# Two layers of windowed attention and experts on one core: another engine for a norm's root, and another way of spreading the score shifts

## The chip, the core and the metric

The kernel runs on one core of a Trainium2 chip. A core has TensorE (matrix products, in the profile PE for the products and PEld for the loading of their stationary operand), VectorE (DVE), ScalarE (ACT), GpSimd (POOL) and SyncE (SP, which here issues DMAs). Each engine works through its own instructions in order; semaphores let one wait for another. SBUF holds the operands, PSUM takes TensorE's results. The metric is the time of one execution on the device in microseconds (us). A kernel's time is the median of several executions, and one more execution is recorded by the hardware profiler.

## The reference: what is computed

The input `x` has 4 sequences of 512 tokens with 128 features. There are two layers, and each computes `x + s * silu(g)` from the normalised input `xn`. `s` comes from attention and `g` from eight experts, of which one is picked for each token.

```python
xn = _layernorm(x)
s = _L0_attn_ref(xn, ...)      # 16 heads of 8, causal window of 64, sigmoid-based weights
g = _silu(_L0_ffn_ref(xn, ...))
x = x + s * g
xn = _layernorm(x)
s = _L1_attn_ref(xn, ...)      # layernorm, blocks of 64 queries by 64 keys, then a feed forward
g = _silu(_L1_ffn_ref(xn, ...))
return x + s * g
```

In layer 1 the attention is cut into windows of 64 tokens that start every 32. Inside a window each of 64 queries sees all 64 keys; neighbouring windows are blended. Its output, projected and with its residual, goes through a second layernorm (`(x - m) / sqrt(v + eps)`), a dense layer to 512 features with gelu, and a dense layer back to 128:

```python
out = ctx @ wproj + bproj + residual
h = layernorm(out, ln2_g, ln2_b)
h = gelu(h @ w1 + b1, approximate=False) @ w2 + b2
return h + out
```

## The kernel before

**Tiles.** A sequence (`b`, four of them) is cut into four tiles of 128 tokens (`t`), so there are 16 attention tiles in each layer. The 16 heads are taken as 4 groups `g` of 32 partitions with 4 heads `j` each. The experts' tokens are sorted into 23 blocks of 128 for each layer.

**Stages and their order.** Every stage is a Python generator (`scores_q`, `queries1`, `scores_k1`, `values1`, `feed1`, the experts' `moe_x`, `moe_h`, `moe_y` and so on). `run` at the end of the function picks the next stage by a simple plan: a stage names the events that it needs (`yield "M", [...]`) and then books what it costs on TensorE and on the other engines (`spent(cost, steps, events)`, with steps such as `("D", 0.7)` for VectorE, `("G", 1.0)` for GpSimd and `(None, 0.9)` for time that belongs to no engine). The plan fixes the order of TensorE's instructions. The order on the other engines follows from the program's order, from a scheduler in the framework with its own costs, and from a few dependencies that `spent` adds where a step follows a GpSimd step. In `run` the plan also remembers a gap before a stage; `bank`, which hands out a PSUM bank, passes it to `awake`, and that fills the gap with products of ones whose result is overwritten. `bank16` hands out a bank for bf16 transpositions without that.

**A norm's root.** `rsqrt` (lines 389 to 393) adds eps on VectorE and takes the power -0.5 on GpSimd. `rsqrt_many` (lines 395 to 408) does the whole on VectorE, by a bit shift for a first guess and three Newton steps; before the change only layer 0's query and key norms (`project0`) use it, with 128 columns. `feed1` (lines 1413 to 1469) runs eight times, for two halves `u` of each sequence. It multiplies the context by `wproj` (`pr`), adds the residual, takes the moments `mv`, the root `rs`, and the normalised rows `hn` on VectorE (`centred`), then adds the row `ffn2` to the residual on GpSimd, transposes `hn` on TensorE (`tr_hn`) and goes on with the two dense layers (`f`, `fy`).

**GpSimd's other work in layer 1.** The gathers of the experts' tokens (`xb`, line 609), the scatters of their results (`yt`, line 666), and the queries masked by head (`q4`, line 1251).

**The shift of layer 1's scores.** The softmax needs each query's maximum subtracted from its scores. `queries1` computes a tile's scores with the queries on the partitions, two window offsets `par` (0 and 32 tokens), and for each the two blocks `w` of 64 queries on partitions `64w` to `64w+63`. VectorE takes the negated maxima `mx` (line 1290) and `split` writes them as a sum of three bf16 terms into `shb` (lines 467 to 472), twelve columns (3 terms by 4 heads) in each group's 32. TensorE transposes `shb` (`tr_sh`), ScalarE copies it out (`shd`, line 1298), and four VectorE products with the 0/1 mask `smask` (line 1301) spread it over the heads: `sh4` has four heads by 128 queries for each `par`. `scores_k1` then computes the scores again with the keys on the partitions, and adds the shifts by products with ones:

```python
for w in range(2):
    for g in range(G):
        r = slice(32 * g, 32 * g + NS * J)
        mm(ps[g // 2][w * KB : (w + 1) * KB, g % 2, par], ones16[r, 0:KB],
           sh4[r, par, :, w * KB : (w + 1) * KB], start=False, stop=True)
```

That is 16 products a tile (2 `par`, 2 `w`, 4 `g`), each with 12 rows and 64 output columns, after 16 products of scores with 32 rows and 64 output columns (each two instructions in the profile). The exponential on ScalarE (`pt`, line 1333) follows. Layer 0 (`scores_k`) shifts its scores with 4 products a tile of 12 rows and 128 output columns.

Of the kernel before, what the change touches and what calls it, by code (L numbers as in the profile page):

```python
# [16 lines left out]
P = 128  # L17
# [3 lines left out]
G, J = 4, 4  # L21
# [36 lines left out]
def two_layers(  # L58
# [336 lines left out]
    def rsqrt_many(dst, src, scale, eps):  # L395

        n = dst.shape[1]
        x = small.tile([P, n], F32, tag="rq_x", name=f"rq_x_{dst.tensor.name}", bufs=1)
        nc.vector.tensor_scalar(x, src, scale, eps, ALU.mult, ALU.add)
        y = small.tile([P, n], F32, tag="rq_y", name=f"rq_y_{dst.tensor.name}", bufs=1)  # L400
        nc.vector.tensor_single_scalar(y.bitcast(I32), x.bitcast(I32), 1, ALU.logical_shift_right)
        nc.vector.tensor_scalar(y.bitcast(I32), y.bitcast(I32), -1.0, float(0x5F3759DF), ALU.mult, ALU.add)
        nc.vector.tensor_scalar_mul(x, x, -0.5)
        z = small.tile([P, n], F32, tag="rq_z", name=f"rq_z_{dst.tensor.name}", bufs=1)
        for i in range(3):
            nc.vector.tensor_tensor(z, y, y, ALU.mult)
            nc.vector.tensor_tensor(z, z, x, ALU.mult)
            nc.vector.scalar_tensor_tensor(dst if i == 2 else y, z, 1.5, y, ALU.add, ALU.mult)
# [50 lines left out]
    def transposed16(src, n, name):  # L459
        ps = bank16(f"tr_{name}")  # L460
        for t in range(n):
            turn(ps[:, t * P : (t + 1) * P], src[:, t], ident16)
        return ps[:, 0 : n * P]
# [446 lines left out]
    for i in range(2):  # L910
        nc.gpsimd.tensor_copy(
            ves[i][:, 0 : H * VC].rearrange("p (h d) -> p h d", d=VC)[:, :, HD], valid[:, i : i + 1].to_broadcast([P, H])
        )
    shbs1 = prepared("shb1_", 2, [P, 2, G, 32], BF16)
    later.close()


# [63 lines left out]
    def scores_q():  # L981

        for i in range(NTILE):
            b, t = divmod(i, NT)
            yield "S", [("k4", b), ("qd", b), ("fit", b - 2)]
            if t == 0:
                mxs[b] = (
                    small.tile([P, NT, H], F32, tag="mx", name=f"mx_{b}"), small.tile([P, NT, H], F32, tag="sm", name=f"sm_{b}")
                )
            mx, sm = mxs[b]  # L990
            qd, k4 = qds[b], k4s[b]


            ps = [banks(f"s0_{b}_{t}_{gg}")[:, :, 0 : J * QW] for gg in range(2)]
            for g in range(G):

                r, eye = (slice(0, P), ident16) if t == 0 else (slice(32 * g, 32 * g + 32), diag32)
                band = band_q[r, 1 if t == 0 else 0, None].to_broadcast([r.stop - r.start, J, QW])
                mm(ps[g // 2][:, g % 2], eye[r], band, start=True, stop=False)
            for c in range(P // QB):  # L1000
                o = t * P + c * QB
                for g in range(G):
                    r = slice(32 * g, 32 * g + 32)
                    mm(
                        ps[g // 2][c * QB : (c + 1) * QB, g % 2], qd[r, o : o + QB], k4[r, :, o : o + QW],
                        start=False, stop=True,
                    )
            def over_keys(dst, src, gg, op):
                nc.vector.tensor_reduce(  # L1009
                    dst[:, t, 8 * gg : 8 * gg + 8].rearrange("p (u j) -> p u j", u=2),  # L1010
                    src.rearrange("p u (j f) -> p u j f", j=J), AX.X, op,
                )

            for gg in range(2):
                over_keys(mx, ps[gg], gg, ALU.max)
                th = att_p.tile([P, 2, J * QW], F32, tag="th", name=f"th_{b}_{t}_{gg}", bufs=2)
                nc.scalar.activation(th, ps[gg], AF.Tanh, scale=0.5 * SCALE)  # L1017
                over_keys(sm, th, gg, ALU.add)
                spent(0 if gg else 1.5, [("D", 0.95), ("A", 0.83), ("D", 0.95)], [("s0", i)], scores=2)
# [218 lines left out]
    def queries1():  # L1238


        for i in range(NTILE):
# [49 lines left out]
                    mx.rearrange("p a g j -> p g a j")[:, 2 * gg : 2 * gg + 2], ps[gg], AX.X, ALU.max, negate=True,  # L1291
                )
            shb = shbs1[i % 2]
            split(shb, mx, f"1_{b}_{t}")
            spent(1.15, [("D", 2.45), ("D", 1.0)], [("s1", i), ("shb", i)], scores=1)
            yield "M", [("shb", i), ("e1", i - 2)]
            shd = att_p.tile([P, 2 * P], BF16, tag="shd1", name=f"shd1_{b}_{t}")
            nc.scalar.copy(shd, transposed16(shb.rearrange("p a g r -> p a (g r)"), 2, f"sh1_{b}_{t}"))
            sh4 = att_p.tile([P, 2, J, P], BF16, tag="sh4_1", name=f"sh4_1_{b}_{t}")
            for j in range(J):  # L1300
                nc.vector.tensor_scalar_mul(sh4[:, :, j], shd.rearrange("p (a f) -> p a f", a=2), smask[:, j : j + 1])  # L1301
            asked1[i] = q4, sh4, v
            spent(0.13, [("A", 0.4), ("D", 1.2)], [("sh1", i)])

    def scores_k1():
        for i in range(NTILE):
            b, t = divmod(i, NT)
            yield "S", [("sh1", i), ("q41", i), ("ov1", i - 1)]
            q4, sh4, v = asked1.pop(i)
            kd, _ = dense[b]  # L1310

            pt = att_p.tile([P, G, 2, J, KB], F32, tag="pt1", name=f"pt1_{b}_{t}", bufs=1)
            ps = [
                banks(f"e1_{b}_{t}_{gg}").rearrange("p u (a j f) -> p u a j f", a=2, j=J) for gg in range(2)
            ]
            for par in range(2):
                for w in range(2):
                    o = par * 2 * HALO + w * KB
                    for g in range(G):
                        r = slice(32 * g, 32 * g + 32)  # L1320
                        mm(
                            ps[g // 2][w * KB : (w + 1) * KB, g % 2, par], kd[r, t * P + o : t * P + o + KB],
                            q4[r, :, o : o + KB], start=True, stop=False,
                        )
                for w in range(2):
                    for g in range(G):
                        r = slice(32 * g, 32 * g + NS * J)
                        mm(
                            ps[g // 2][w * KB : (w + 1) * KB, g % 2, par], ones16[r, 0:KB],
                            sh4[r, par, :, w * KB : (w + 1) * KB], start=False, stop=True,  # L1330
                        )
            for gg in range(2):
                nc.scalar.activation(pt[:, 2 * gg : 2 * gg + 2], ps[gg], AF.Exp, scale=SCALE)  # L1333
            pts1[i] = pt, v
            spent(1.45, [("Ae", 1.03), ("Ae", 1.03)], [("e1", i)], scores=2)
# [77 lines left out]
    def feed1():  # L1413


        for b in range(B):
            for u in range(0, NT, 2):
# [13 lines left out]
                nc.vector.tensor_tensor(res[:, two], ps, res[:, two], ALU.add)  # L1431
                mv = moments(res[:, two], f"d{b}_{u}")
                rs = small.tile([P, 2], F32, tag="rs", name=f"rs_d{b}_{u}")
                rsqrt(rs, mv[:, :, 1], LN_EPS)
                centred(hn[:, two], res[:, two], mv, rs)
                spent(1.0, [("D", 0.7), ("D", 0.7), ("G", 1.0), ("D", 0.7)], [("pr", b, u)])
                nc.gpsimd.tensor_tensor(
                    res[:, two], res[:, two], row("ffn2")[:, None, :].to_broadcast([P, 2, D]), ALU.add
                )
# [122 lines left out]
```

## Time and profile before

| what | value |
|---|---|
| median of 3 runs | 506.65 us (503.2 to 510.5) |
| the profiled execution, its own time | 499.03 us |
| its span, first to last instruction | 497.3 us |
| TensorE busy | 417.3 us, 84% |
| VectorE busy | 337.5 us, 68%, 1013 instructions |
| ScalarE busy | 261.6 us, 53% |
| GpSimd busy | 179.7 us, 36% |
| mean granted TensorE clock | 0.918 |
| power -0.5 on GpSimd (L393, 128x2) | 8 instructions, 742 ns each |
| masked products of the shifts (L1301, 128x256 bf16) | 64 instructions, 283 ns each |
| shift products in layer 1 (12 rows, 64 columns, 256 streamed) | 256 instructions, 283 ns each |

A row of the profile's groups reads: line, engine, operation, output<-input by the program's names, shapes, count, then busy time and mean duration, then how long the engine stood idle before these instructions and what released it. The duration of one TensorE product includes its way through the array, so products that run side by side have durations that overlap; what a stage costs is read from start to start. A row of the timeline is start, duration, engine, line, operation, names and shapes, and in brackets the idle time before it with what ended it.

Layer 1's attention runs from about 227 us (the first `mx`, L1290) to the end, beside layer 1's experts, whose gathers start at 331.0 us and whose last scatter starts at 469.4 us.

### The profile page before, as it was taken

The numbers are of one execution on the slowest core, as the hardware profiler recorded it, in microseconds if no ns is written. First come the engines' busy times: TensorE is split into PE (matmuls) and PEld (weight loads), VectorE is DVE, ScalarE is ACT, GpSimd is POOL, SyncE is SP. The second block draws the span as 40 slices with busy tenths as digits, with TensorE's granted clock in tenths as the row PEclk, the third lists the DMA queues.
The fourth block names the chain that finished last, engine by engine and source line by source line (L and its number), as shares of the span: only waits on it lengthen the run. The fifth ranks groups of instructions, "written<-read, shape, count | busy, mean of one in ns | idle before, by whom it ended". The sixth has DMA issues, their size and how long they took to land.

```text
span 497.3 us, 14720 instructions
## 1 busy us (share of the span) xinstructions
PE 417.3 (84%) x5663; PEld 295.0 (59%) x5663; DVE 337.5 (68%) x1013; ACT 261.6 (53%) x513; POOL 179.7 (36%) x251
## 2 busy tenths in 40 slices
PE   5876897998899696599999896878999994699985
PEld 2642565676565462345655574646879883588863
DVE  6899997553846958958774584884677761475565
ACT  1422665697567534375555655444676442246622
POOL 5741455346522222233320304136352335642311
PEclk8787699999999967779999998998999998599999
DMA  5405454756243010100000000051453773352032
GB/s 170 130 1 135 111 156 114 211 152 202 50 109 96 12 54 22 43 22 3 3 22 3 3 1 22 2 150 30 130 140 102 176 200 100 109 134 77 19 105 66
DMA packets 61894, 42.12 MB, mean 85 GB/s; under 512 B 11328, under 2 KB 54208, under 8 KB 61824
## 3 DMA queue, kind: packets, MB, share of 16 engines
q1 hardware_dynamic: 58464, 34.85, 25.3%
q0 software_dynamic: 2944, 6.04, 4.5%
q8 instruction: 45, 0.74, 0.6%
q10 hardware_dynamic: 416, 0.29, 0.3%
q14 instruction: 25, 0.20, 0.1%
HBM read 34.99 MB, written 6.16 MB: 83 GB/s over the span
## 4 chain that ended last, share of the span: by engine, by line
PE 47%; DVE 27%; issue 9%; ACT 7%; POOL 5%; DMA 3%; SPq 0%; POOLq 0%; ACTq 0%; DVEq 0%
PE e L83 8%; PE h L83 6%; PE s L83 5%; PE y L83 4%; PE ov L83 4%; DVE mx L1009 3%; DVE mx L1290 3%; PE fy L83 3%; PE f L83 2%; ACT th L1017 2%; PE o L88 2%; ACT pt L1106 2%; PE qkv L83 1%; PE v L83 1%; DVE sm L1009 1%
## 5 line engine op out<-in xcount | busy, mean ns | idle before, releaser
L666 POOL DMA_INDIRECT yt<-yb,put_at x46 | 46.1, 1002 | 104.3 <-DVE yb L664 24.8
L609 POOL DMA_INDIRECT xb<-xd,tokens_at x46 | 46.2, 1004 | 53.9 <-DVE tokens_at L586 17.1
L83 PE MATMUL y<-wb,hb 128*128 128x128 f32 x368 | 49.7, 285 | 4.3 <-ACT hb L696 3.2
L83 PE MATMUL h<-xbT,wb 128*128 128x128 f32 x368 | 51.2, 291 | 2.3 <-ACT xbT L344 1.3
L83 PEld LDWEIGHTS h<-xbT,wb 128*128 128x128 f32 x368 | 46.5, 202 | 8.5 <-issue 3.3
L83 PEld LDWEIGHTS y<-wb,hb 128*128 128x128 f32 x368 | 46.1, 198 | 7.7 <-ACT hb L696 3.9
L83 PE MATMUL e<-q,kd 32*64 32x256 f32 (+1 forms) x864 | 44.9, 457 | 0.4 <-ACT pt L1106 0.4
L1017 ACT ACTIVATE th<-s 128x768 f32<-128x768 f32 x32 | 26.0, 813 | 29.8 <-DVE mx L1009 29.2
L1333 ACT ACTIVATE pt<-e 128x1024 f32<-128x1024 f32 x32 | 31.0, 1021 | 19.9 <-PE e L83 19.8
L1290 DVE TENSOR_REDUCE mx<-s 128x16 f32<-128x1024 f32 x32 | 37.6, 1218 | 4.4 <-PE s L83 4.2
L83 PE MATMUL s<-k,qd 32*32 32x384 f32 (+1 forms) x1024 | 37.2, 484 | 2.6 <-ACT pt L1333 2.3
L1106 ACT ACTIVATE pt<-e 128x1024 f32<-128x1024 f32 x32 | 31.0, 1021 | 14.2 <-PE e L83 14.1
L83 PEld LDWEIGHTS <-ones 12*64 12x64 bf16 (+2 forms) x439 | 21.5, 107 | 28.6 <-issue 20.4
L1009 DVE TENSOR_REDUCE mx<-s 128x8 f32<-128x768 f32 x32 | 29.3, 949 | 11.9 <-PE s L83 11.9
L344 ACT COPY osb<-ov 128x512 f32<-128x512 f32 x33 | 18.6, 587 | 26.8 <-PE ov L83 21.4
L696 ACT ACTIVATE hb<-h,bb 128x128 f32<-128x128 f32 x92 | 26.5, 382 | 11.3 <-PE h L83 10.2
L1009 DVE TENSOR_REDUCE sm<-th 128x8 f32<-128x768 f32 x32 | 30.0, 946 | 1.3 <-ACT th L1017 1.0
L83 PE MATMUL ov<-pt,va 64*32 64x128 f32 (+1 forms) x896 | 28.8, 290 | 0.4 <-DVE ctx L344 0.2
L83 PEld LDWEIGHTS e<-q,kd 32*64 32x64 f32 x864 | 19.4, 139 | 11.5 <-issue 6.4
L1251 POOL TENSOR_TENSOR q<-qd,jmask 128x640 f32<-128x640 f32 x16 | 20.0, 1260 | 14.7 <-PE e L83 13.4
L83 PE MATMUL e<-sh,ones 12*64 12x256 bf16 (+1 forms) x320 | 20.8, 311 | 3.6 <-DVE sh L1301 3.6
L704 ACT ACTIVATE hb<-h,bb 128x128 f32<-128x128 f32 x56 | 15.8, 376 | 14.7 <-PE h L83 12.0
(287 smaller groups left out, 898.1 us busy)
## 6 DMA issues: line engine op xcount, KB each, us to landing
wb<-in_w SPq DMA_DIRECT2D x92, 256.0 KB
bb<-in_b SPq DMA_DIRECT2D x46, 64.0 KB
acc<-yt SPq DMA_DIRECT2D x8, 256.0 KB
xd<-ln_a SPq DMA_DIRECT2D x4, 256.0 KB
xd<-xr SPq DMA_DIRECT2D x4, 256.0 KB
out<-acc SPq DMA_DIRECT2D x8, 128.0 KB
x<-in_x SPq DMA_DIRECT2D x3, 256.0 KB
bb<-in_cols SPq DMA_DIRECT2D x46, 2.0 KB
```

Source lines behind the costliest of these rows:

```text
L83: ins = nc.tensor.matmul(*args, **kw)
L344: (nc.scalar.copy if e == "A" else nc.vector.tensor_copy)(dst, src)
L609: nc.gpsimd.indirect_dma_start(out=xb, out_offset=None, in_=xd, in_offset=bass.IndirectOffsetOnAxis(ap=tokens_at[:, k : k + 1], axis=0),)
L666: nc.gpsimd.indirect_dma_start(out=yt, out_offset=bass.IndirectOffsetOnAxis(ap=routed[n][0][:, k : k + 1], axis=0), in_=y, in_offset=None,)
L696: nc.scalar.activation(h[:, c, :], src[:, c * P : (c + 1) * P], AF.Gelu, bias=bias[:, c : c + 1])
L704: nc.scalar.activation(dst, src_c, AF.Relu, bias=b)
L1009: nc.vector.tensor_reduce(dst[:, t, 8 * gg : 8 * gg + 8].rearrange("p (u j) -> p u j", u=2), src.rearrange("p u (j f) -> p u j f", j=J), A ...
L1017: nc.scalar.activation(th, ps[gg], AF.Tanh, scale=0.5 * SCALE)
L1106: nc.scalar.activation(pt[:, 2 * gg : 2 * gg + 2], ps[gg], AF.Exp)
L1251: engine.tensor_tensor(dst, src[:, None, o : o + TW].to_broadcast([P, J, TW]), jmask[:, :, None].to_broadcast([P, J, TW]), ALU.mult,)
L1290: nc.vector.tensor_reduce(mx.rearrange("p a g j -> p g a j")[:, 2 * gg : 2 * gg + 2], ps[gg], AX.X, ALU.max, negate=True,)
L1333: nc.scalar.activation(pt[:, 2 * gg : 2 * gg + 2], ps[gg], AF.Exp, scale=SCALE)
```

## The change

Two parts. In `feed1` the root is taken by `rsqrt_many`, that is by 13 VectorE instructions on 2 columns in place of one VectorE and one GpSimd instruction; the booked steps change from two VectorE steps, one GpSimd step and one VectorE step to two VectorE steps, 0.9 us of no engine and one VectorE step. `rsqrt_many`'s tiles get a fixed size, so that both uses share them.

In layer 1's shifts the two query blocks `w` are laid on different rows of one group, 16 rows for each, so that one product serves both. `split` writes into `terms`; VectorE multiplies `terms` by `own` (1 where a partition belongs to block `c`) into `shb`; a product with `fold` (two identity matrices of 64 rows, one above the other) takes the place of the transposition, with 64 columns in place of 128 and a bank from `bank`; `shd` and `sh4` become half as wide; and the product with `lane` (1 where a row's block is the output column's block) has 32 rows and 128 output columns. 16 products a tile become 8. Seven VectorE instructions build the four constants in `scores_q`, at layer 0's tile 6.

```diff
     def rsqrt_many(dst, src, scale, eps):
         n = dst.shape[1]
-        x = small.tile([P, n], F32, tag="rq_x", name=f"rq_x_{dst.tensor.name}", bufs=1)
+        x = small.tile([P, P], F32, tag="rq_x", name=f"rq_x_{dst.tensor.name}", bufs=1)[:, 0:n]
...
+            if i == 6:
+                half = small.tile([P, 2, 2], F32, tag="half", name="half", bufs=1)
+                nc.vector.tensor_reduce(half[:, 0], ident.rearrange("p (w q) -> p w q", w=2), AX.X, ALU.add)
+                nc.vector.tensor_copy(own, half[:, 0])
+                nc.vector.tensor_tensor(fold, ident16[:, 0:KB], ident16[:, KB:P], ALU.add)
+                nc.vector.tensor_reduce(
+                    smask1, ident.rearrange("p (g s j) -> p j g s", g=2 * G, j=J)[:, :, :, 0:NS], AX.XY, ALU.add
+                )
+                nc.vector.tensor_reduce(half[:, 1], ident.rearrange("p (g c r) -> p c g r", g=G, c=2), AX.XY, ALU.add)
+                nc.vector.tensor_copy(lane.rearrange("p (c k) -> p c k", c=2), half[:, 1, :, None].to_broadcast([P, 2, KB]))
+                traced(skip=True)
...
             shb = shbs1[i % 2]
-            split(shb, mx, f"1_{b}_{t}")
+            terms = small.tile([P, 2, G, NS * J], BF16, tag="terms", name=f"terms_{b}_{t}", bufs=1)
+            split(terms, mx, f"1_{b}_{t}")
+            nc.vector.tensor_tensor(
+                shb.rearrange("p a g (c r) -> p (a g) c r", c=2)[:, :, :, 0 : NS * J],
+                terms.rearrange("p a g r -> p (a g) r")[:, :, None].to_broadcast([P, 2 * G, 2, NS * J]),
+                own[:, None, :, None].to_broadcast([P, 2 * G, 2, NS * J]), ALU.mult,
+            )
             spent(1.15, [("D", 2.45), ("D", 1.0)], [("s1", i), ("shb", i)], scores=1)
             yield "M", [("shb", i), ("e1", i - 2)]
-            shd = att_p.tile([P, 2 * P], BF16, tag="shd1", name=f"shd1_{b}_{t}")
-            nc.scalar.copy(shd, transposed16(shb.rearrange("p a g r -> p a (g r)"), 2, f"sh1_{b}_{t}"))
-            sh4 = att_p.tile([P, 2, J, P], BF16, tag="sh4_1", name=f"sh4_1_{b}_{t}")
+            shd = att_p.tile([P, 2, KB], BF16, tag="shd1", name=f"shd1_{b}_{t}")
+            ps = bank(f"sh1_{b}_{t}")[:, 0 : 2 * KB].rearrange("p (a f) -> p a f", a=2)
+            for par in range(2):
+                mm(ps[:, par], shb[:, par].rearrange("p g r -> p (g r)"), fold, start=True, stop=True)
+            nc.scalar.copy(shd, ps)
+            sh4 = att_p.tile([P, 2, J, KB], BF16, tag="sh4_1", name=f"sh4_1_{b}_{t}")
             for j in range(J):
-                nc.vector.tensor_scalar_mul(sh4[:, :, j], shd.rearrange("p (a f) -> p a f", a=2), smask[:, j : j + 1])
+                nc.vector.tensor_scalar_mul(sh4[:, :, j], shd, smask1[:, j : j + 1])
...
-                for w in range(2):
-                    for g in range(G):
-                        r = slice(32 * g, 32 * g + NS * J)
-                        mm(
-                            ps[g // 2][w * KB : (w + 1) * KB, g % 2, par], ones16[r, 0:KB],
-                            sh4[r, par, :, w * KB : (w + 1) * KB], start=False, stop=True,
-                        )
+                for g in range(G):
+                    r = slice(32 * g, 32 * g + 32)
+                    mm(ps[g // 2][:, g % 2, par], lane[r], sh4[r, par], start=False, stop=True)
...
                 rs = small.tile([P, 2], F32, tag="rs", name=f"rs_d{b}_{u}")
-                rsqrt(rs, mv[:, :, 1], LN_EPS)
+                spent(1.0, [("D", 0.7), ("D", 0.7)], [("mv", b, u)])
+                rsqrt_many(rs, mv[:, :, 1], 1.0, LN_EPS)
                 centred(hn[:, two], res[:, two], mv, rs)
-                spent(1.0, [("D", 0.7), ("D", 0.7), ("G", 1.0), ("D", 0.7)], [("pr", b, u)])
+                spent(0, [after(("mv", b, u)), (None, 0.9), ("D", 0.7)], [("pr", b, u)])
```

## The prediction

> **What bounds the kernel now.** I read the page first, then the table of waits, then the timeline around the longest wait, then TensorE's timeline of single attention tiles. The page says that no engine is full, that TensorE carries most of the chain that ended last, and VectorE most of the rest.
>
> ```profile
> PE 417.3 (84%) x5663; PEld 295.0 (59%) x5663; DVE 337.5 (68%) x1013; ACT 261.6 (53%) x513; POOL 179.7 (36%) x251
> PE 47%; DVE 27%; issue 9%; ACT 7%; POOL 5%; DMA 3%; SPq 0%; POOLq 0%; ACTq 0%; DVEq 0%
> ```
>
> By stretches, TensorE is busy 52.0 of 55 us from 345 to 400 and 44.4 of 45 from 428 to 473, but 16.1 of 28 between them. The table of waits names the hole (total, times, longest): the normalised rows `hn` wait for GpSimd's root in every feed-forward half, and once for 14.6 us.
>
> ```profile
> DVE hn L428 <- POOL rs_d L393: 21.9, 8, 14.6
> ...
> PE tr_hn L88 <- DVE hn L428: 13.8, 3, 11.8
> ```
>
> The timeline of that place (start, duration, engine, line, operation, idle before it):
>
> ```profile
> 410.93 0.16 DVE L392 TENSOR_SCALAR rs_d<-mv_d 128x2 f32<-128x2 f32 x1
> ...
> 418.41 2.48 POOL L1251 TENSOR_TENSOR q<-qd,jmask 128x640 f32<-128x640 f32 x2
> ...
> 425.92 0.74 POOL L393 TENSOR_TENSOR rs_d<-rs_d,neghalf 128x2 f32<-128x2 f32 x1
> 426.70 0.60 DVE L428 TENSOR_SCALAR hn<-xr,mv_d,rs_d 128x128 f32<-128x128 f32 x2 [14.57 <-POOL rs_d L393]
> 427.19 0.66 PE L88 MATMUL tr_hn<-ident,hn 128*128 128x128 f32 x2 [11.76 <-DVE hn L428]
> ```
>
> The root's input is ready at 411.1. GpSimd reaches it at 425.92, since four scatters, three gathers and two masked queries stand ahead of it from 412.49 on, and a scatter waits for the one before it to land. VectorE stands behind `hn`, and TensorE behind its transposition.
>
> **The root by VectorE.** Out go an add (166 ns) and GpSimd's power (742 ns), in come 13 VectorE instructions on 2 columns, nearly all dependent. Their price is read from a dependent chain of small operations in the trace, 32 columns wide:
>
> ```profile
> 364.79 0.17 DVE L468 CAST shb<-mx 128x32 bf16<-128x32 f32 x1
> 364.99 0.19 DVE L470 TENSOR_TENSOR rest<-mx,shb 128x32 f32<-128x32 f32 x1
> 365.22 0.18 DVE L471 CAST shb<-rest 128x32 bf16<-128x32 f32 x1
> ```
>
> Starts lie 0.20 to 0.23 apart, so I take 12 x 0.21 + 0.12 (one instruction is independent) = 2.65 us from the first to `hn`. The last half shows today's price with GpSimd idle: 1.05 us.
>
> ```profile
> 485.69 0.17 DVE L392 TENSOR_SCALAR rs_d<-mv_d 128x2 f32<-128x2 f32 x1
> ...
> 486.74 0.60 DVE L428 TENSOR_SCALAR hn<-xr,mv_d,rs_d 128x128 f32<-128x128 f32 x2 [0.89 <-POOL rs_d L393]
> ```
>
> Where GpSimd is free the change therefore loses 1.6 us, and it adds 8 x 12 instructions that VectorE must issue in order. The eight places:
> - 411: `hn` could be done by 414.9 (2.65 us of root, and three shift products between). TensorE ends its queued products at 415.4, then has a transposition and one block's second layer, until about 417.1. The next scores need the masked queries, on GpSimd at 418.41 to 420.9; the first is ready at 419.7, where TensorE now starts at 430.2. That is 10.4 us. The tokens of 422.36 and 423.64 take a median 3.5 us to land, so their transposition can be at 427 instead of 436.8 (9.8 us); the gather of 438.45 lets only 8.9 through, as it lies behind three scatters some 4.4 us apart, which the change doesn't speed. In the tail the gates' first product stands ahead of the root and waits for the last scatter, which I get 7 to 8 us earlier. I take -8.6, between -6 (scatters stay 5 us apart) and -14.4 (11.8 of idle time and 2.6 of slow clock behind it, the bound without GpSimd).
> - 276, 298, 336, 360: +1.6, +1.8, +0.9, +0.9; the last two are less because the root already waited behind a gather and a scatter. At 276 the eviction behind `hn` holds TensorE 1.28 us, at 298 layer 1's second norm hangs behind it. At 336 and 360 blocks of experts cover part. Ends 0 and +5.2; I take +3.3.
> - 464, 476, 486: +0.6, +1.7, +1.6 = +3.9. Nothing covers the last two: TensorE waits 1.26 and 0.75 us for `hn` there already. Its waits become 2.9 and 2.4. After 3.55 us of idle time (at 305.84) the next eight transpositions took 1.91 instead of 1.04 us; after 2.05 us (at 324.34) the scores took their usual 1.1. The Trainium skill ("TensorE: Matmul & The Clock Gate", What's actually happening) puts the gate at an idle window of about 3.4 us. By both these waits stay below it: nothing added, up to 3 us if a window falls badly.
>
> `res += ffn2` stays on GpSimd behind `hn`, so gathers queued behind it see the same +0.9 at 336, counted above.
>
> **The shift by one product.** VectorE: the four products on half the columns. 512 columns take 492 ns and 256 take 283, so 128 take about 180, and four in a row 0.52 instead of 0.87 us. The added product by `own`, 192 columns, lies between 128 columns (283 ns) and 368 (532): 0.35 us. Sum zero (-0.1 to +0.15 a tile). The copy on ScalarE goes from 376 to about 280 ns, and the two small products stream 64 columns, not 128: -0.03 us a tile, -0.5 over 16 tiles.
>
> On TensorE 16 products of 64 output columns become 8 of 128. Do they get cheaper? In layer 1 now (8 products of 256 columns, tile 12 x 64, between products of tile 32 x 64):
>
> ```profile
> 449.01 0.69 PE L83 MATMUL e<-q,kd 32*64 32x256 f32 x16
> 449.49 0.32 PE L83 MATMUL e<-sh,ones 12*64 12x256 bf16 x8
> 449.60 0.75 PE L83 MATMUL e<-q,kd 32*64 32x256 f32 x16
> ```
>
> The eight take 0.11 us: they run side by side. Four of 128 columns fill the same array for the same 0.11 us, so nothing is gained, and the eight weight loads that go were hidden beside products anyway. But layer 0 has the tile shape that the change brings in:
>
> ```profile
> 96.43 0.43 PE L83 MATMUL e<-bands_k,diag 32*32 32x512 bf16 x16
> 96.79 1.12 PE L83 MATMUL e<-q,kd 32*64 32x512 f32 x24
> 97.84 0.39 PE L83 MATMUL e<-sh,ones 12*128 12x512 bf16 x4
> 98.17 0.44 PE L88 MATMUL xt<-ident,xb 128*128 128x128 f32 x2
> ```
>
> Scaled from layer 1 by columns, bands and shifts should take 0.22 each and the scores 4 x 0.22 = 0.88; they take 0.36, 0.33 and 1.05. The excess of 0.11 to 0.17 us comes at each change of tile shape. A rule speaks for this reading and against the change: the Trainium skill ("TensorEngine Tiling (Array Packing)", Key Properties) says that changing the tiling mode drains TensorE, while moving between tiles of one mode does not. Layer 1's scores and shifts now have one mode (32 x 64); after the change they go 64, 128, 64, 128. By layer 1's row alone the stage costs nothing more, by rule and layer 0's rows 0.17 + 0.12 + 0.17 = 0.46 us a tile, 7.4 over 16 tiles. I take the latter, two thirds of it on the path, since TensorE is near full from 345 to 400 and from 428 to 473 and has gaps elsewhere: +4.9 (0 to +9).
>
> Three small ones: the shifts' bank now passes through `awake`, which fills planned gaps; a filler takes 0.2 us, and 7 of 16 tiles wait there now (3.5 us in all), so +0.6 (-0.5 to +2). The seven new constants in layer 0's sixth tile make about 1.4 us of VectorE once, partly in its gaps: +0.5 (0 to +1.4). 110 more instructions to fetch: 0 to +1.
>
> **Sum:** -8.6 + 3.3 + 3.9 - 0.5 + 4.9 + 0.6 + 0.5 = +4.1 us on the profiled 499.03 (span 497.3 and 1.7 around it), so about 503.1. That execution lies 7.6 below the median; carried to it, 510.7.
>
> **Rivals.** (1) The stall is worth all of its 14.4 us and the shape changes are hidden: -14.4 + 3.3 + 3.9 + 1 = -6 on the sum, some 500; with the four early roots covered too, 497. For it: the hole is the largest in the trace. Against: masked queries at 419.7 and gathers at 438.45 don't move. 0.13. (2) Slower: the changes of tile shape, in the scores of layer 1. With each at 0.23 us and all 16 tiles on the path they cost 11, and the sum is +10, 517. The sum without them is -0.8, so they make the kernel slower from 0.05 us a tile on, and measurably from 0.68. For it: TensorE's 98% from 428 to 473; against: waits for GpSimd after 411 absorb two or three tiles. 0.22. (3) The change doesn't do what it says: GpSimd's backlog, not the root, sets the pace, and TensorE waits for queries and tokens instead; the stall gives back 4, the sum is +9, about 515. 0.12. The forecast has 0.53.
>
> **Numbers.** A difference under 2% (10 us) can't be told from none here. From these cases: faster 0.07, same 0.69, slower 0.24. The range takes in rival 3 and the near halves of 1 and 2: 500 to 519.
>
> **What would show it.** No wait of `hn` for GpSimd; TensorE's hole at 411 to 427 down to about 3 us, ended by masked queries; 2.5 to 2.8 us from the moments to `hn`; the stretch from the first scores of a tile in layer 1 to what follows it at 1.8 us, not 1.39; TensorE's waits for `hn` in the tail at 2 to 3 us. I am wrong if the hole stays or moves whole to another wait, if the scores' stretch stays at 1.4, or if VectorE's order around the root is a different one.

## The result, and the profile after

The changed kernel takes 520.36 us (517.07 to 522.48, 4 runs) where the kernel before took 505.59 on the same chip: a ratio of 1.029 (95% interval 1.0235 to 1.0336). Repeated later it was 1.017 (1.008 to 1.026) on a chip where before takes 510.1 us and 1.021 (1.015 to 1.027) on one where it takes 494.4. The forecast, 510.7 on 506.65, was 1.008: right in sign, about a third to a half of the size. Medians here are of all runs and ratios of those within 1.5% of the kernel's fastest, so that a ratio can differ by some thousandths from that of the medians beside it.

Two lines of the changed kernel's profile, from the chip of the first result: the engines' busy times and (from the table of waits: total, times, longest) TensorE's waits for the normalised rows.

```profile
PE 435.6 (84%) x5537; PEld 296.5 (57%) x5537; DVE 358.7 (69%) x1131; ACT 260.6 (50%) x513; POOL 174.9 (34%) x243
PE tr_hn L88 <- DVE hn L428: 9.3, 4, 3.6
```

VectorE has 21 us and 118 instructions more. TensorE is busy 18 us longer with 126 products fewer, so its products ran slower or were fed worse. The page's chain of work that ended last accounts for a quarter of the span only, so it isn't read further. `hn` waited 21.9 us for GpSimd before; that row is gone, as is the wait of 11.8 us behind it.

This profile can't be set against the one of before, though, and the first thing to learn is why. The same table has rows that before has nowhere:

```profile
PE s L83 <- issue: 3.9, 2, 3.1
PE ov L83 <- issue: 3.0, 9, 0.4
```

TensorE stands still there, and the profile shows nothing that it waits for. All nine profiles taken on the chips on which before takes 505 to 510 us, of the changed kernel and of edits, have such waits, 4 to 15 us of them; none of the ten from the two chips where it takes 494 to 496 has any, the changed kernel's and before's own included. Part of this is only the label: the longest one stands in the profiles of all chips. Here it is in the first result and in the changed kernel on a chip of 494 us:

```profile
50.74 0.50 PE L83 MATMUL s<-band_q,diag 32*128 32x384 bf16 x2 [3.11 <-issue]
```

```profile
52.09 0.50 PE L83 MATMUL s<-band_q,diag 32*128 32x384 bf16 x2 [3.11 <-ACT th L1034]
```

With this wait and the one of 0.83 us behind it taken off, 4 to 11 us of "issue" are left on the slower chips, in single waits of 0.2 to 1.2 us. From here on the parts of the time are taken from a pair on one chip without them: before (span 492.1) and after (span 507.5; this execution took 509.2, the longest of six; that kernel's median there is 504.8, and before's 494.4). The shift alone is from the same chip. The root alone is from the other chip of this kind, where before's own profile (span 492.0) differs from this one by up to 0.9 us in a stretch. Lags are read from the starts of the same stage on TensorE, whose order of stages is the same in both:

| stretch, by before's time | forecast | both parts | shift alone | root alone |
|---|---|---|---|---|
| layer 0 and earlier, to 223 | +0.5 | +1.8 | +0.4 | -1.1 |
| layer 1 to the scores of the old hole, 223 to 409 | +7.7 | +8.6 | +5.8 | +0.2 |
| the old hole, 409 to 436 | -8.6 | -5.9 | -1.1 | -7.9 |
| 436 to 468 | +1.2 | +5.0 | +0.6 | +2.2 |
| tail, 468 to the end | +3.3 | +6.0 | 0 | +8.4 |
| sum | +4.1 | +15.4 | +5.7 | +1.8 |

The forecast column is the prediction's terms put in their stretches. Of the 11.3 us between it and this execution, 4.4 are the execution's own distance from its median. The rest is spread: most between the hole and the tail, then the hole and the tail themselves; and this execution with both parts lost more than the sum of the parts, 7.5. That both cost more than their sum as a rule isn't shown: by the ratios on this chip both together are 1.021 (1.015 to 1.027), and the parts 1.016 and 1.001.

The old hole in TensorE's timeline of that profile (start, duration, engine, line, operation, idle time before it):

```profile
421.88 0.38 PE L88 MATMUL tr_hn<-ident,hn 128*128 128x128 f32 x2
...
425.06 0.69 PE L83 MATMUL e<-q,kd 32*64 32x256 f32 x16 [1.52 <-POOL q L1268]
425.68 0.29 PE L83 MATMUL e<-sh,lane 32*128 32x256 bf16 x4
425.90 0.69 PE L83 MATMUL e<-q,kd 32*64 32x256 f32 x16
426.52 0.29 PE L83 MATMUL e<-sh,lane 32*128 32x256 bf16 x4
426.74 0.33 PE L88 MATMUL xt<-ident,xb 128*128 128x128 f32 x1
...
434.33 0.30 PE L88 MATMUL xt<-ident,xb 128*128 128x128 f32 x1 [2.65 <-DMA xb<-xd,tokens_at]
```

`hn` is there without a wait. What ends last now is the masked query, and then the gathered tokens behind the scatters: the two things the prediction named. The middle lines show one tile's scores, 425.06 to 426.74: 1.68 us. Before has 1.39, here between the first scores of a tile and what follows them:

```profile
443.74 0.69 PE L83 MATMUL e<-q,kd 32*64 32x256 f32 x16
...
445.13 0.44 PE L88 MATMUL xt<-ident,xb 128*128 128x128 f32 x2
```

In the tail TensorE waited 1.26 us before:

```profile
472.42 0.58 PE L88 MATMUL tr_hn<-ident,hn 128*128 128x128 f32 x2 [1.26 <-DVE hn L428]
```

Now VectorE and TensorE read

```profile
480.22 0.16 DVE L399 TENSOR_SCALAR rq_x_rs_d<-mv_d 128x2 f32<-128x2 f32 x1
...
480.80 0.28 DVE L1409 TENSOR_TENSOR att<-o,rec 128x128 f32<-128x128 f32 x1
...
481.40 0.42 DVE L1502 TENSOR_TENSOR acc<-acc,x 128x256 f32<-128x256 f32 x1
...
483.77 0.60 DVE L428 TENSOR_SCALAR hn<-xr,mv_d,rs_d 128x128 f32<-128x128 f32 x2
484.17 0.73 PE L88 MATMUL tr_hn<-ident,hn 128*128 128x128 f32 x2 [3.60 <-DVE hn L428]
```

The root takes 3.55 us from its first instruction to `hn`, not 2.65, because products of attention and of the experts' sum stand between its steps on VectorE: seven instructions, three of them shown. In the 3.5 us behind the wait TensorE's granted clock is 0.50.

### The profile page after: what moved, and what is told of

The parts are those of the page before. It is cut to its first block, busy times and chain, and to the rows that moved or that the text cites. A ratio compares the mean times of both kernels' runs of the same rounds, so it can differ in the third digit from the quotient of the medians.

```text
span 518.9 us, 14574 instructions
## 1 busy us (share of the span) xinstructions
PE 435.6 (84%) x5537; PEld 296.5 (57%) x5537; DVE 358.7 (69%) x1131; ACT 260.6 (50%) x513; POOL 174.9 (34%) x243
## 5 line engine op out<-in xcount | busy, mean ns | idle before, releaser
L83 PE MATMUL e<-q,kd 32*64 32x256 f32 (+1 forms) x864 | 49.0, 456 | 2.4 <-issue 1.6
L83 PE MATMUL ov<-pt,va 64*32 64x128 f32 (+1 forms) x896 | 33.5, 304 | 3.9 <-issue 3.0
L83 PEld LDWEIGHTS <-ones 128*128 128x128 bf16 (+1 forms) x185 | 14.6, 105 | 23.7 <-issue 16.3
L83 PEld LDWEIGHTS e<-q,kd 32*64 32x64 f32 x864 | 17.7, 137 | 17.4 <-issue 11.3
L83 PEld LDWEIGHTS ov<-pt,va 64*32 64x32 f32 (+1 forms) x896 | 19.0, 111 | 13.0 <-issue 7.6
```

Of the source, the lines that this page charges most:

```text
L83: ins = nc.tensor.matmul(*args, **kw)
```

## The experiments

**The two parts alone.** The question after the first result was whether the shift or the root made most of its 14.8 us.

`e1_root_only`: the root of the change, the shift as before.

```diff
-                rsqrt(rs, mv[:, :, 1], LN_EPS)
+                spent(1.0, [("D", 0.7), ("D", 0.7)], [("mv", b, u)])
+                rsqrt_many(rs, mv[:, :, 1], 1.0, LN_EPS)
```

> The kernel before with only the root of the feed forward moved to VectorE; the shifts are as before. Theory A (the shifts carry the loss: three changes of tile shape in every tile of scores, and the product by own on TensorE's wait): the root gives back the hole at 411 (about -10 us) and loses about 6 in the tail and 3 at the early roots, so it is within 1% of before, 0.99 to 1.01, and TensorE's wait for the shifts' terms stays at some 3.5 us. Theory B (the root carries the loss, by 96 more VectorE instructions and waits of TensorE behind them): 1.02 to 1.03. Theory C (any changed program shifts TensorE's code fetches against the weights' transfers): a scatter that goes with neither part, with stalls of TensorE without a releaser in the values' products.

Measured 495.99 us, ratio 1.001 (0.998 to 1.004). The hole's gain of 7.9 us is paid back, 2.2 us at once and 8.4 in the tail.

`e1_shift_only`: the shift's half of the diff with its constants, the root as before.

> The kernel after with the root back on GpSimd; only the shifts are changed. Theory A: 16 tiles at 0.29 us more for the scores (4.7 us) and some 5 us more of waiting for the terms behind the product by own, so 1.015 to 1.025, and the hole at the root of the fifth feed-forward half is there again. Theory B: 1.00, within 0.5%. Theory C: as likely slower as the other part alone.

Measured 501.72 us, 1.010 (1.005 to 1.016); once more as `e3_shift_only_again` further down, 1.016. That lies between theory B's 1.00 and theory A's 1.015 to 1.025, and neither part alone makes the first result's 1.029.

`e1_shift_cols64`: the shift alone, but each product with `lane` cut in two of 64 output columns, so that the tile's width stays that of the scores.

```diff
-                    mm(ps[g // 2][:, g % 2, par], lane[r], sh4[r, par], start=False, stop=True)
+                    for w in range(2):
+                        mm(ps[g // 2][w * KB : (w + 1) * KB, g % 2, par], lane[r, w * KB : (w + 1) * KB], sh4[r, par], ...)
```

> As the run with only the shifts changed, but the product with lane is cut into two of 64 output columns (16 products a tile instead of 8), so that scores and shifts have one tile shape again. Theory A: the scores of a tile fall from 1.68 back to about 1.4 us, 4.7 us less over 16 tiles, so about 0.99 of the run with only the shifts changed. If the number of products mattered and not the shape: the scores stay at 1.68 or grow.

Measured 500.91 us, 1.0115 (1.005 to 1.018). The stage of scores is back at 1.39 us, so the changes of width do cost 0.29 us a tile. The whole time doesn't move measurably, against theory A: those 4.6 us over 16 tiles are mostly hidden. From the start of layer 1 to the end the profile lost 3.9 us here and 6.3 in the shift alone on the same chip: about 2.4 us are the widths, by two single profiles.

`e1_root_one`: the root by VectorE in the half of the old hole only, everything else as before.

```diff
+                if (b, u) == (2, 0):
+                    rsqrt_many(rs, mv[:, :, 1], 1.0, LN_EPS)
+                else:
                     rsqrt(rs, mv[:, :, 1], LN_EPS)
```

> The kernel before with the root by VectorE in one of the eight feed-forward halves only, the fifth (third sequence, first half), where before VectorE waited 14.6 us for GpSimd. Theory A: the hole goes and nothing is lost in the tail, so 0.975 to 0.99. Theory B, or if the hole only moves to another wait of TensorE (queries or tokens from GpSimd): 0.995 to 1.005.

Measured 489.81 us, 0.984 (0.975 to 0.994). This beats both kernels: it keeps the gain and touches no tail. The two parts made 1.001 x 1.010 = 1.011 where both together had measured 1.029, which the next groups take up.

**Together again.** `e2_after_again` is the changed kernel unedited.

> The changed kernel once more, beside the other three of this group. The two parts measured alone were 1.001 and 1.010 of the kernel before, their sum is 1.011, and both together measured 1.029. Theory S (the parts add up and the rest was that chip or that group of runs): 1.008 to 1.016, and no waits of TensorE that end with 'issue'. Theory I (the parts together do something that neither does alone): 1.024 to 1.034, with some 10 us of waits of TensorE that end with 'issue' again, and a loss of over 8 us between the scores near 347 us and those near 412 us.

Measured 1.017 (1.008 to 1.026), with 9.5 us of issue waits. The interval holds neither theory off. Theory I's issue waits were there, which theory S had excluded.

`e2_after_root_one`: the changed kernel with the root by VectorE in the half of the hole only (edit as in `e1_root_one`).

> The shift as changed, the root by VectorE in one half only, the first of the third row of the batch, where TensorE stood still for 10 us before; GpSimd has the other seven as before. Theory S: the shift costs 1.010 and this root gains 0.016, so 0.99 to 1.00. Theory I, if the roots of the early halves make the loss between 347 and 412 us: 0.99 to 1.00 too, but without the loss there and without TensorE's issue waits. Theory I, if the shift and its larger constants or the different instruction stream make it by themselves: 1.01 to 1.02, with the issue waits still there.

Measured 0.9996 (0.997 to 1.002), with 11.5 us of issue waits and the loss between 347 and 412 us. So the early and late roots make neither, and all roots but one cost 1.8% together with the shift.

`e2_after_cols64`: the changed kernel with the products cut as in `e1_shift_cols64`.

> The changed kernel with the shift's products cut into two of 64 columns each, twice as many but of the tile width of the scores around them, so that the tile width doesn't change inside a stage. Alone this took the stage of scores from 1.68 back to 1.39 us a tile and the time not at all. Theory T (where TensorE is the bound, changes of width cost their 0.29 us a tile also in time): 1.00 to 1.01 below the changed kernel's ratio, that is 3 to 5 us faster than it. Theory S or I without tile widths: within 0.5% of the changed kernel. If TensorE's issue waits come from how many instructions it has to fetch, they grow here, and the kernel is slower than the changed one by 0.5 to 1%.

Measured 1.0085 (1.004 to 1.013). Against 1.017 of the changed kernel that speaks for theory T, but the two intervals overlap; 128 more products bring 15.0 us of issue waits without making it slower.

`e2_after_root_six`: the changed kernel with the root of the last two halves back on GpSimd (`if b < 3:` around the new root).

> The changed kernel with the root of the last two halves (the fourth row of the batch) back as before, with GpSimd between VectorE's two ends; six halves keep the root by VectorE. Theory of the prediction (the tail's two waits for the normalized row grow by 1.6 us each and nothing covers them): 3.3 us faster than the changed kernel, up to 6 with the slow clock that follows the longer wait, so a ratio 0.006 to 0.012 below it. Rival (the tail waits for the scatters in any case): no difference to the changed kernel. Nothing before 460 us should differ.

Measured 1.010 (1.007 to 1.014), 0.007 below the changed kernel: the expected size, inside the interval of the latter.

**Chip or change?** The issue waits had appeared with both parts and with neither alone, but on different chips. `e3_before_again` is before unedited.

> The kernel before once more, with a profile from the same chip as the other three. All five profiles of kernels with both parts show 9 to 15 us of waits of TensorE that end with 'issue', at the same places (3.11 us at 50 us, then near 344, 408 and 455); the profiles of before and of the four kernels of the first group show none, but they come from other chips, on which before takes 495 to 499 us and not 505 to 510. Theory K (it is the chip, not the change): on a chip where before takes over 503 us, this profile shows the same issue waits, 8 to 12 us of them; on one where it takes under 500, none here and none in the changed kernel. Theory I (it is the change): none here on any chip.

493.77 us, a chip without these waits. `e3_after_third` is the changed kernel beside it.

> The changed kernel beside the kernel before's own profile. Theory K: its issue waits are those of before on this chip, to 2 us, and its ratio is that of the parts, 1.01 to 1.017. Theory I: 9 to 10 us of issue waits whatever before shows, and 1.02 to 1.03.

Measured 504.76 us, 1.021 (1.015 to 1.027), and not one issue wait. The ratio lies above theory K's 1.010 to 1.017, which its interval still touches. Theory I of the change as the cause of the waits falls: the same program has them on one chip and not on the other. The loss between the scores of 347 and of 412 us, 12.5 us in the first result's profile against one of before from elsewhere, is 3.9 us in this pair. Why that stretch is dearer on the slower chips stays open: there the eight profiles with the shift lose 6 to 19 us in it, and `e4_root_tail` further down, without the shift, 4.7. That before has the issue waits too on those chips isn't shown, as no profile of before came from one. Its own times, 11 to 16 us longer there, suggest it, and so does `e4_root_tail`: its program differs from before's only in the last two halves of the feed forward, and it has 9.3 us of them, all ahead of these.

`e3_root_one_again` and `e3_shift_only_again` repeat two kernels of the first group.

> The root by VectorE in one half only, no change of the shift; 0.984 (0.975 to 0.994) in the first group. Theory K: 0.98 to 0.99 here too, whatever the chip. If the gain comes only where the rest of the kernel runs without issue waits, 0.99 to 1.00.

Measured 490.62 us, 0.9875 (0.977 to 0.998): the gain stands on a second chip.

> The shift alone, 1.010 (1.005 to 1.016) in the first group. Theory K: 1.005 to 1.016 again, and the issue waits of before. Theory I: no issue waits, as in the first group.

Measured 500.85 us, 1.016 (1.008 to 1.023), without issue waits.

**What of the shift costs.** The waits of TensorE for the shift's terms, before and in the shift alone:

```profile
PE tr_sh L88 <- DVE shb L472: 3.7, 8, 0.9
```

```profile
PE sh L83 <- DVE shb L1313: 7.6, 9, 1.8
```

They double, by 3.9 us. Nearly half of that is one wait of 1.77 us, in the timeline of the shift alone:

```profile
252.31 1.29 POOL L1425 TENSOR_TENSOR xr<-xr,projb 128x512 f32<-128x512 f32 x1 [4.52 <-DMA xd<-xr]
252.38 1.90 DVE L1268 TENSOR_TENSOR k<-kd,jmask 128x640 f32<-128x640 f32 x1
...
254.35 1.04 POOL L1086 TENSOR_TENSOR q<-q2d,wmask 128x512 f32<-128x512 f32 x1 [0.75 <-PE e L83]
254.48 0.95 DVE L471 CAST terms<-rest 128x32 bf16<-128x32 f32 x1
...
255.75 0.36 DVE L1313 TENSOR_TENSOR shb<-terms,own 128x192 bf16<-128x192 bf16 x1
256.17 0.23 PE L83 MATMUL sh<-fold,shb 128*128 128x64 bf16 x2 [1.77 <-DVE shb L1313]
```

The same place before:

```profile
249.99 1.27 POOL L1402 TENSOR_TENSOR xr<-xr,projb 128x512 f32<-128x512 f32 x1 [2.90 <-DMA xd<-xr]
...
251.67 0.82 DVE L1251 TENSOR_TENSOR k<-kd,jmask 128x640 f32<-128x640 f32 x1
...
252.68 0.13 DVE L471 CAST shb<-rest 128x32 bf16<-128x32 f32 x1
```

The keys' product takes 0.82 us before and 1.90 after, the cast 0.13 and 0.95. Each of the two stretched instructions begins inside a GpSimd product; the short one ends 0.04 us after GpSimd's, the long one 0.68 after. So the two engines hardly share: the later one does most of its work when the other has ended. The Trainium skill ("SBUF — State Buffer", Who interferes with whom) says so: a VectorE instruction with two SBUF inputs excludes a GpSimd instruction that reads SBUF, a copy, cast or scalar product in a two-port mode excludes any GpSimd instruction, each for a whole instruction, and a reduction takes no part. The traces agree: among the stretched instructions there are products, casts and scalar products, and no reduction (the longest reductions, `mx`, read PSUM, so that says little). From 225 us on, the VectorE instructions that took over 0.3 us more than the median of their line and shape lost 3.8 us in 6 of them before, 7.8 in 11 in the shift alone, 10.3 in 10 in the root alone and 12.3 in 14 with both; all of these run beside a GpSimd product. These are VectorE's losses; how much of them reaches the kernel's time they don't show.

`e4_shift_no_own` leaves the added product out, so that the second block of queries gets no shift.

```diff
-            split(terms, mx, f"1_{b}_{t}")
-            nc.vector.tensor_tensor(shb..., terms..., own..., ALU.mult)
+            split(shb, mx, f"1_{b}_{t}")
```

> The shift alone, but the product by own is left out: the three terms are written straight into the first half of the columns, so the second block of queries gets no shift and the output is not the reference's. Everything else of the shift stays (fold, lane, narrower masks, TensorE's products). Theory W (what costs is VectorE's added product, which stands ahead of the products that TensorE waits for, while the narrower masks that were to pay for it come behind them): TensorE's waits for the shift's terms fall from 7.6 to 3 to 4.5 us, and the ratio from 1.010 to 1.016 (shift alone) to 0.999 to 1.005. Rival T (tile widths, lane weights or the layout cost it): waits fall, the ratio stays at 1.008 or more.

Measured 1.014 (1.0075 to 1.0205). The waits fell to 5.5 us, the ratio didn't, which is what rival T expected; this chip has issue waits, and `e5_shift_no_own` below is the same kernel on one without.

`e4_shift_own_twice` does it twice.

```diff
+            for _ in range(2):
                 nc.vector.tensor_tensor(shb..., terms..., own..., ALU.mult)
```

> The shift alone with the product by own done twice, the same values written again. Theory W: TensorE's waits for the terms grow from 7.6 to 10 to 12 us, and the ratio from 1.010 to 1.016 to 1.017 to 1.026. Rival T, or VectorE has room there: 1.009 to 1.016.

Measured 1.025 (1.018 to 1.031), by the ratios 5.5 us above the kernel without the product on the same chip, and waits larger than theory W's 10 to 12 us:

```profile
PE sh L83 <- DVE shb L1314: 19.1, 11, 4.9
```

VectorE's chain to `shb` is on the path: two products of 0.36 us in 16 tiles are 11.5 us of VectorE, and about half of that is time.

`e4_shift_no_projb` leaves out the GpSimd addition of the lines above.

```diff
-                nc.gpsimd.tensor_tensor(xrs[b], xrs[b], projb[:, None, :].to_broadcast([P, NT, D]), ALU.add)
```

> The shift alone with GpSimd's addition of the projection's bias row to the residual left out (4 products of 128x512, 1.29 us each; the output is not the reference's). In the shift's trace the keys' product on VectorE at 252.38 took 1.90 us and not 0.82, and the cast at 254.48 0.95 and not 0.17, each while a GpSimd product ran, and TensorE waited 1.77 us for the terms there. Theory L (VectorE's and GpSimd's products hold each other up, and this is where the shift's longer chain loses most): the keys' product in that place takes 0.82 again, TensorE's wait there falls under 0.6, and the ratio to 1.004 to 1.011. Rival (the stretch has another cause, such as the order on VectorE): 1.90 and 1.77 us stay.

Measured 1.014 (1.0025 to 1.025), which is no smaller than the shift alone elsewhere; the time says nothing. The place does:

```profile
258.42 0.82 DVE L1268 TENSOR_TENSOR k<-kd,jmask 128x640 f32<-128x640 f32 x1
...
259.96 0.36 DVE L1313 TENSOR_TENSOR shb<-terms,own 128x192 bf16<-128x192 bf16 x1
```

The keys' product takes 0.82 us again and TensorE doesn't wait there at all (1.77 before the edit). But at 428 us another keys' product takes 2.85 us beside GpSimd, and TensorE waits 3.71. The collision is gone in one place and stands in another: theory L is right on the mechanism, and what removing one instance is worth in time isn't measured.

`e5_before_third` and `e5_shift_no_own` are before, and the shift without the product by `own`, on one chip.

> The kernel before, for its profile on this chip. Kernels have now run on five chips: on two, before takes 494 to 495 us and no profile has a wait of TensorE that ends with 'issue'; on the others it takes 505 to 510, and all nine profiles of changed kernels have 4 to 15 us of them. If this is one of the slow ones: theory K (a property of the chip) expects 4 to 10 us of issue waits in before's own profile, the first of them near 50 us, and a loss of 4 to 8 us against the fast chips' profile between 343 and 408 us; if the change makes them, none. If it is a fast one, none, and a span of 490 to 495.

493.68 us and no issue waits: this is again one of the 494 us chips, so whether before has them on the others stays open.

> The shift without the product by own, 1.014 (1.0075 to 1.0205) in the last group, beside before's own profile. On a chip without issue waits, where the whole shift measured 1.010 and 1.016: theory W (own's product makes at least half of the shift's cost) 1.001 to 1.007; rival T (tile widths, layout or the copy make it) 1.009 to 1.015. On a chip with issue waits: 1.008 to 1.018[...].

Measured 499.89 us, 1.009 (1.005 to 1.013): it meets rival T's range, not W's, and lies only 0.001 below the whole shift on this chip, with an interval of 0.004 and more on each. TensorE's waits for the terms are back at 3.8 us, and from layer 1 to the end the profile loses 2.5 us against 6.3 with the product on the same chip. So two single profiles give the product most of the loss there, and the times don't confirm it. The other 4.5 us of this profile lie ahead of layer 1, where the shift changes only the seven constants. The whole shift lost 4.4 us there in its profile on this chip and 0.4 on the other one, so most of it isn't a fixed cost of the constants: up to layer 1 the granted clock was 0.86 in both profiles of this chip and 0.89 in that one, against 0.88 for before. Why the clock was lower stays open.

**The tail.** `e4_root_tail`: the root by VectorE in the last two halves only (`if b == 3:`).

> The kernel before with the root by VectorE in the last two halves only. Prediction's price: 1.7 + 1.6 = 3.3 us, ratio 1.005 to 1.008. Theory Q (other VectorE work stands between the root's steps in the first of the two, and the clock falls behind TensorE's wait of over 3 us): 5 to 8 us, ratio 1.010 to 1.016, with a wait for the normalized row of 3.4 to 3.8 us and slow products behind it. Rival (the tail waits for the scatters in any case): 1.000 to 1.003. Nothing ahead of 460 us differs from before.

Measured 514.73 us on 506.58, 1.013 (1.006 to 1.021): by the ratio 6.8 us, and 5.8 from 468 us to the end in the profile, against before's from another chip. Its first wait:

```profile
490.00 0.73 PE L88 MATMUL tr_hn<-ident,hn 128*128 128x128 f32 x2 [3.60 <-DVE hn L428]
```

Theory Q holds: the same 3.60 us as with the whole change, and in the 3.5 us behind it the granted clock is 0.50 and the products take 1.8 times as long.

## Why the prediction was wrong

**The hole** was read rightly: GpSimd's place in the root goes, TensorE waits for masked queries and tokens instead, and 7.9 us come out of it with the root alone (8.6 forecast), 5.9 with both parts.

**The tail is the priced step that failed.** "464, 476, 486: +0.6, +1.7, +1.6" was worked out from the root's 12 instructions standing alone on VectorE, and "by both these waits stay below it: nothing added". Alone the root does take no more than the forecast 2.65 us: 2.37 in the last half of the first profile. In the half before, VectorE's queue puts seven other instructions between the steps, the wait is 3.60 us instead of 2.9, and the granted clock is 0.50 behind it. The two halves cost 6 to 8 us, 3.3 were forecast. The range's "up to 3 us if a window falls badly" was the true case.

**"Sum zero" for VectorE in the shift failed too, and a second error hid it.** The product by `own` has its size (0.36 us, 0.35 forecast). The saving that was to pay for it doesn't: four masked products in a row went from 0.87 us to 0.74, where 0.52 was forecast. Before and the shift alone:

```profile
349.33 0.87 DVE L1301 TENSOR_SCALAR sh<-shd,smask 128x256 bf16<-128x256 bf16 x4
```

```profile
354.18 0.74 DVE L1328 TENSOR_SCALAR sh<-shd,smask 128x128 bf16<-128x128 bf16 x4 [0.23 <-ACT shd L1324]
```

The price came from a mean, 492 ns for 512 columns. Of those 16 products 13 took 339 to 353 ns, and three that ran beside GpSimd products 0.55, 0.65 and 2.21 us. With the medians, 343 and 279 ns, the same line through 512 and 256 columns gives 247 ns for 128, and 247 is the median measured. So VectorE has 0.23 us a tile more, not zero. And the product stands ahead of what TensorE waits for, while the narrower masks come behind. That it costs time is shown by doing it twice or not at all, 5.5 us apart for two products. For one, two single profiles of one chip give 3.8 us and the times there 0.5, give or take 3. The changes of tile width, put at 0.46 us a tile and +4.9, are 0.29 us a tile and, by two profiles, about +2.4. So it is luck that the shift's sum of 5.0 us came near the 5 to 8 measured: both terms were wrong, and part of the loss may lie in layer 0.

**What the forecast had no term for** is that VectorE's and GpSimd's products stop each other. It is not shown to be why this execution with both parts lost more than their sum: what the stretched instructions lose with both, 8.5 us above before, is less than the two parts' 4.0 and 6.5, and 2.5 us of the excess lie ahead of layer 1. In two places the rows show it at work. At 360 us the root's steps and then a cast that GpSimd held up (0.76 instead of 0.17 us) make TensorE's wait for the terms 2.17 us; with either part alone it is 1.3. At 445:

```profile
445.19 1.28 POOL L1268 TENSOR_TENSOR q<-qd,jmask 128x640 f32<-128x640 f32 x1
445.24 1.91 DVE L1268 TENSOR_TENSOR k<-kd,jmask 128x640 f32<-128x640 f32 x1
...
448.45 0.23 PE L83 MATMUL sh<-fold,shb 128*128 128x64 bf16 x2 [2.40 <-DVE shb L1313]
```

Before, TensorE waited 0.2 us here, and in the 3.5 us behind the wait the granted clock is now 0.58. This is the stretch that was forecast at +1.2 and lost 5.0. That the collision causes the wait is read from these rows and from its like at 252 us, where one was taken out; no run took this one out.

**Early roots,** +3.3, are +0.2 us to 409 us with the root alone, or +1.1 against before's profile from its own chip. Rival 2 gave the time nearest to the first result, 517, by the wrong mechanism. The base was mixed as well: the profile of 499.03 was from an execution without issue waits, 7.6 us below the median that it was carried to, most likely from another chip.

Of the signs asked for, three were there: no wait of `hn` for GpSimd, the hole ended by masked queries after 1.5 us, the scores' stretch at 1.68 us (1.8 forecast). The other two failed at the tail: the root took 3.55 us to `hn` there (2.5 to 2.8; over the eight halves it is 2.4 to 5.6), and of the waits of 3.60 and 2.07 us the first is too long (2 to 3). The prediction had named the reason as a sign of being wrong: another order on VectorE around the root.

## What to carry to other kernels

Price an instruction that is added to an in-order engine by what stands around it in that engine's queue and by who waits behind it, not by its own time: a saving behind the wait doesn't pay for an addition ahead of it. Move a helper's work only where the helper is late: here one of eight places made the whole gain (0.984 and 0.9875 by itself), and the tail, where nothing covers, took it back. A price read from a mean over equal instructions can hold a few stretched ones: look at the median too. Before two profiles are compared, see that they come from chips with the same time for the same kernel, and see whether a wait with a new label isn't the old one.

## What was not expected of the hardware

- Two chips run before in 494 to 496 us without a single wait of TensorE under "issue", others in 505 to 510, where the changed kernel and its edits show 4 to 15 us of them. The longest, 3.11 us near 50 us in six of nine profiles, stands in the other chips' profiles too and is put down to ScalarE there. The rest is mostly in waits of 0.2 to 0.5 us, many of them near 340, 400 and 450 us. What TensorE waits for in them no run shows.
- A VectorE product or cast that meets a GpSimd product ends after it: 0.82 becomes 1.9 us, 0.18 becomes 0.95.
- TensorE's clock fell after shorter waits than the prediction supposed. The granted clock in the 3.5 us behind a wait was 0.56 after 1.77 us (at 256.17, the shift alone), 0.52 after 2.17, 0.58 after 2.40 and 0.65 after 2.65. But it was 1.00 after 2.07 us in the tail, and 1.00 after 3.09 us (at 469.5, `e3_root_one_again`). The length of the last wait alone doesn't decide, and the window of about 3.4 us that the prediction took from the Trainium skill ("TensorE: Matmul & The Clock Gate", What's actually happening) is no safe bound here.
